# The load of W's first chunk: issued by ScalarE beside the first tile, in place of second on SyncE

## The chip, the cores and the metric

The kernel runs on one core of a Trainium2 chip. The metric is the device time of one execution in microseconds, as the median of several runs. The core has five engines that each follow their own list of instructions: TensorE (PE in the profile, with its weight loads as PEld), VectorE (DVE), ScalarE (ACT), GpSimd (POOL) and SyncE (SP), which here only issues transfers. Transfers between HBM and SBUF are carried by 16 DMA engines.

## The reference

The inputs are x (4 rows of 1024 positions with 512 features, f32), a condition of 256 numbers for each row, a matrix W of 1536 x 512 and a bias b of 512.

```python
def reference(x, cond, W, b):
    hidden = concat([cond, cond], -1)                      # (4, 512)
    x_mean = mean(x, axis=1, keepdims=True)                # (4, 1, 512)
    fused = concat([x, x_mean * ones, hidden[:, None] * ones], -1)
    return x + relu(einsum('bld,do->blo', fused, W) + b)
```

W has three parts of 512 rows. The first multiplies x itself, the second the mean over the positions, the third the condition. The last two give one vector for each of the four rows of x, which acts as a bias.

## The kernel before

**Tiling.** x is cut into 32 tiles of 128 positions, eight for each of the four rows. The part of W that multiplies x is cut into four chunks of 128 rows (j = 0 to 3). A chunk is a load of 256 KB: 128 partitions of 512 f32 numbers, one W row of 2 KB for each partition, and chunk j takes every fourth row beginning with row j. Tile 0 and tile 1 of x are also loaded alone, 256 KB each.

**Products.** Each operand is split in two numbers of a shorter type, a high part and what is left (hi and lo of x, w_hi and w_lo of W), and each tile takes three products for each chunk: hi by w_hi, lo by w_hi, hi by w_lo. So a tile needs 12 matmuls of 128 x 512 (L594), which add up in one PSUM bank.

**What the first tiles need.** Tiles of the first row of x are transposed by TensorE (`turn`, L427, four transposes for tile 0), then ScalarE makes hi (`split_hi`, L440) and VectorE makes lo (`split_lo`, L455) and the sums for the mean (`add_up`, L450). For each chunk of W, ScalarE or VectorE makes w_hi (`split_w_hi`, L398 or L400), and VectorE makes w_lo from it (`split_w_lo`, L403). Later rows of x are loaded in another layout (z, L334) and transposed by VectorE (L429).

**Order.** A planner (`Plan`) holds every step as a task with a cost on each engine that may do it, what it depends on and its due time. It draws an order for all engines by a search with a fixed seed and then emits each task in that order. All loads and stores are tasks of SyncE. The first loads have a fixed order in a list (`first_loads`):

```python
        (("x", 0, 0), 0.8, lambda e: load_x(0, 0, 1)),
        (("w", 0), 1.5, lambda e: load_w(0)),
        (("x", 0, 1), 1.0, lambda e: load_x(0, 1, 1)),
        (("w", 1), 0.9, lambda e: load_w(1)),
        (("w", 2), 0.7, lambda e: load_w(2)),
        (("w", 3), 0.7, lambda e: load_w(3)),
        (("x", 0, 2), 1.6, lambda e: load_x(0, 2, 2)),
```

Then follow the condition, b, tiles 4 to 7 of x in one load of 1 MB, and the z loads. In short, x0 and x1 here mean tiles 0 and 1 of x, and w0 to w3 the four chunks.

**Before the planned work.** Ahead of the planner's order the code emits some instructions by hand: VectorE clears a tile for warming (L266), ScalarE runs one Relu (L270), which brings the load of its function table with it, and TensorE multiplies zeros five times (`fill`, L278). More such fills are put in where the planner sees TensorE wait in the opening.

**Buffers.** x0 to x3 share one buffer of the pool `xpool` (five buffers, tag "x"), and the four chunks of W share the next one, `w_x`. Both are taken from the pool by the first load that writes them.

Of the kernel before, what the change touches and what calls it, by code (L numbers as in the profile page):

```python
# [9 lines left out]
F32 = mybir.dt.float32  # L10
# [201 lines left out]
def kernel(  # L212
# [8 lines left out]
    nc = tc.nc  # L221
    B, L, D = x.shape
    H = cond.shape[1]
    P = 128
    Q = 32
    NQ = P // Q
    J = D // P
# [5 lines left out]
    G = 4  # L233
# [12 lines left out]
    xpool = ctx.enter_context(tc.tile_pool(name="xpool", bufs=X_BUFS))  # L246
# [15 lines left out]
    Wv = W.rearrange("(s p j) o -> s p j o", p=P, j=J)  # L262
# [3 lines left out]
    nc.vector.memset(warm, 0.0)  # L266
    one = const.tile([P, 1], F32, name="one")
    nc.vector.memset(one, 1.0)
    table_warm = const.tile([P, 1], F32, name="table_warm")
    nc.scalar.activation(table_warm, one, AF.Relu)  # L270
    ident = const.tile([P, P], F32, name="ident")
# [41 lines left out]
    xs, zs, w_src = {}, {}, {}  # L313
# [3 lines left out]
    def load_x(g, i=0, n=G):  # L317
        r, k = divmod(g * G, NK)
        if not i:
            xs[g] = xpool.tile([P, G, D], F32, tag="x", name=f"x{g}")  # L320
        nc.sync.dma_start(out=xs[g][:, i : i + n], in_=xv[r, :, k + i : k + i + n, :])  # L321

    def x_tile(t):
# [14 lines left out]

    def load_w(j):
        if not j:  # L340
            w_src["x"] = xpool.tile([P, J, D], F32, tag="x", name="w_x")
        nc.sync.dma_start(out=w_src["x"][:, j, :], in_=Wv[0, :, j])

    def load_cond():
        w_src["cond"] = xpool.tile([P, 2, KH, D], F32, tag="x", name="w_cond")
# [5 lines left out]
    MB = 2.66  # L351
    first_loads = [
# [7 lines that stand above are left out]
        (("c",), 0.05, lambda e: nc.sync.dma_start(out=c_sb, in_=cond)),  # L360
        (("b",), 0.05, lambda e: nc.sync.dma_start(out=b_sb[0:1, :], in_=b.rearrange("(o d) -> o d", o=1))),
# [34 lines left out]
    def split_w_hi(e, j):  # L396
        if e == "act":
            nc.scalar.activation(w_hi[:, j, :], w_src["x"][:, j, :], AF.Copy)  # L398
        else:
            nc.vector.tensor_copy(w_hi[:, j, :], w_src["x"][:, j, :])  # L400

    def split_w_lo(e, j):
        nc_of[e].tensor_tensor(  # L403
            w_lo[:, j, :], w_src["x"][:, j, :], w_hi[:, j, :].bitcast(F32), ALU.subtract
        )

    for j in range(J):
        plan.add(("w_hi", j), {"act": (0.54, 0.63), "dve!": (0.37, 0.43)}, [("w", j)],
                 lambda e, j=j: split_w_hi(e, j))
        plan.add(("w_lo", j), {"dve!": (0.6, 0.69)}, [("w_hi", j)],  # L410
                 lambda e, j=j: split_w_lo(e, j))
# [323 lines left out]
```

## Time and profile before

| | before |
|---|---|
| median of 3 runs | 107.79 us (107.71 to 110.29) |
| the profiled execution's own time | 107.62 us |
| its span in the profile | 105.8 us |
| TensorE busy | 100.4 us (95%), 450 matmuls |
| VectorE, ScalarE, GpSimd busy | 79.9, 53.4, 63.8 us |
| moved by DMA | 26.31 MB, 249 GB/s over the span |
| granted TensorE clock | 1.0 in all 40 slices |

The span runs from the first to the last instruction that the profiler saw; 1.8 us of the execution's own time lie outside it. Lines such as L594 are lines of the kernel's file. SPq stands for the part of SyncE that issues transfers. A group's "busy" adds up its instructions, and the idle time after it is that of the engine just before them, with what ended it.

### The profile page before, as it was taken

Reading aid. Unit: us, or ns where it says so; the run is one execution under the profiler, and the core shown is the slowest. Engines: PE = TensorE matmul, PEld = TensorE weight load, DVE = VectorE, ACT = ScalarE, POOL = GpSimd, SP = SyncE. Lnnn points to the kernel's source line nnn. Section 1 sums busy time; section 2 is a strip of 40 time slices with the busy share of each in tenths; the row PEclk is TensorE's granted clock in tenths of the full one; section 3 lists DMA queues with packets and bytes.
Section 4 is the critical chain, followed back from the end, with each engine's and each line's share of the span. In section 5 each row is a group of like instructions: output and inputs, shape, how many; then the busy total and the mean of one; then the engine's idle time right before and its main releaser. Section 6 shows DMA issues by size and latency. Waiting matters only on the chain.

```text
span 105.8 us, 1452 instructions
## 1 busy us (share of the span) xinstructions
PE 100.4 (95%) x450; PEld 80.1 (76%) x450; DVE 79.9 (76%) x118; ACT 53.4 (50%) x121; POOL 63.8 (60%) x58
## 2 busy tenths in 40 slices
PE   5969999999999999999999999999999999999970
PEld 2447888888878878888878878888788788888860
DVE  1089154499999979999988999999998960488360
ACT  5253383572557482698665724776466220384000
POOL 6000000264040499999999999999999994087000
PEclk9999999999999999999999999999999999999999
DMA  2799999999999999992499999995699984004932
GB/s 108 180 386 396 270 204 286 427 271 201 266 299 192 201 202 201 200 293 96 163 239 253 330 392 390 390 405 212 218 264 345 349 318 184 20 6 192 344 147 104
DMA packets 22945, 26.31 MB, mean 249 GB/s; under 512 B 1173, under 2 KB 13721, under 8 KB 22810
## 3 DMA queue, kind: packets, MB, share of 16 engines
q1 hardware_dynamic: 22938, 26.23, 87.5%
q8 instruction: 3, 0.05, 0.2%
q14 instruction: 4, 0.03, 0.1%
HBM read 17.83 MB, written 8.39 MB: 248 GB/s over the span
## 4 chain that ended last, share of the span: by engine, by line
PE 89%; DMA 4%; DVE 2%; ACT 1%; SPq 0%; issue 0%
PE po_None L594 82%; DMA w_x<-in_L_cond_W_dram 4%; PE po L594 3%; PE xT L427 3%; PE pb L534 1%; PE pb L535 1%; DVE w_lo L403 1%; ACT w_hi L398 1%; DVE sums L450 1%; PE po L586 0%; DVE o L620 0%; SPq L321 0%; DVE w_hi L400 0%; PE pt L496 0%
## 5 line engine op out<-in xcount | busy, mean ns | idle before, releaser
L594 PE MATMUL po_None<-w_hi,hi 128*128 128x512 f32 x124 | 49.0, 399 | 1.0 <-ACT w_hi L398 0.7
L594 PE MATMUL po_None<-w_lo,hi 128*128 128x512 f32 x124 | 49.1, 399 | 0.0
L594 PE MATMUL po_None<-w_hi,lo 128*128 128x512 f32 x124 | 48.4, 397 | 0.0
L615 POOL TENSOR_TENSOR o<-o,x 128x512 f32<-128x512 f32 x27 | 34.7, 1317 | 4.5 <-ACT o L612 4.5
L594 PEld LDWEIGHTS po_None<-w_hi,hi 128*128 128x128 f32 x124 | 23.3, 188 | 7.2 <-ACT w_hi L398 1.4
L594 PEld LDWEIGHTS po_None<-w_lo,hi 128*128 128x128 f32 x124 | 23.3, 188 | 5.4 <-DVE w_lo L403 0.2
L440 ACT ACTIVATE hi<-xT 128x512 fp32r<-128x512 f32 (+1 forms) x34 | 19.8, 582 | 15.0 <-PE xT L427 8.1
L594 PEld LDWEIGHTS po_None<-w_hi,lo 128*128 128x128 f32 x124 | 23.3, 188 | 5.2
L429 DVE STREAM_TRANSPOSE xT<-z 128x512 f32<-128x512 f32 x24 | 25.5, 1093 | 1.4 <-POOL lo L455 1.4
L612 ACT ACTIVATE o<-o 128x512 f32<-128x512 f32 x30 | 17.9, 627 | 8.4 <-DVE o L609 3.9
L455 DVE TENSOR_TENSOR lo<-xT,hi 128x512 fp32r<-128x512 f32 (+1 forms) x22 | 14.0, 635 | 10.6 <-ACT hi L440 10.3
L455 POOL TENSOR_TENSOR lo<-xT,hi 128x512 fp32r<-128x512 f32 x12 | 15.5, 1299 | 9.5 <-ACT hi L440 9.5
L609 DVE TENSOR_TENSOR o<-po_None,bias 128x512 f32<-128x512 f32 x23 | 14.8, 680 | 7.0 <-ACT bias L539 4.7
L506 POOL TENSOR_TENSOR wc<-w_cond 128x512 f32<-128x512 f32 x2 | 2.6, 1298 | 18.2 <-DMA w_cond<-in_L_cond_W_dram 18.2
L520 DVE SCALAR_TENSOR_TENSOR acc<-w_mean,tot,acc 128x512 f32<-128x512 f32 x16 | 12.0, 751 | 0.4
L609 POOL TENSOR_TENSOR o<-o,bias 128x512 f32<-128x512 f32 x8 | 10.3, 1303 | 0.7 <-ACT bias L539 0.7
L605 ACT ACTIVATE o<-po_None 128x512 f32<-128x512 f32 x8 | 4.8, 596 | 6.1 <-PE po_None L594 6.1
L509 DVE SCALAR_TENSOR_TENSOR acc<-wc,cT,acc 128x512 f32<-128x512 f32 x8 | 5.9, 740 | 0.9 <-ACT acc L517 0.8
L427 PEld LDWEIGHTS xT<-ident,x 128*128 128x128 f32 x32 | 5.5, 205 | 1.3 <-issue 0.7
L440 ACT ACTIVATION_READ_ACCUMULATOR hi<-xT 128x1 f32 x32 | 6.2, 193 | 0.0
L526 ACT ACTIVATE acc_hi<-acc 128x512 fp32r<-128x512 f32 x4 | 2.4, 600 | 6.9 <-DVE acc L520 6.9
L539 ACT ACTIVATE bias<-pb 128x512 f32<-128x512 f32 x4 | 2.4, 600 | 6.8 <-PE pb L535 6.8
(44 smaller groups left out, 48.7 us busy)
## 6 DMA issues: line engine op xcount, KB each, us to landing
out_dram<-o SPq DMA_DIRECT2D x31, 256.0 KB, 3.9
x<-in_x_dram SPq DMA_DIRECT2D x7, 1024.0 KB, 8.4
z<-in_x_dram SPq DMA_DIRECT2D x24, 256.0 KB, 8.3
w_x<-in_L_cond_W_dram SPq DMA_DIRECT2D x4, 256.0 KB, 4.8
w_cond<-in_L_cond_W_dram SPq DMA_DIRECT2D x1, 1024.0 KB, 10.1
w_mean<-in_L_cond_W_dram SPq DMA_DIRECT2D x1, 1024.0 KB
x<-in_x_dram SPq DMA_DIRECT2D x2, 256.0 KB, 4.5
x<-in_x_dram SPq DMA_DIRECT2D x1, 512.0 KB, 6.0
```

Of the source, the lines that this page charges most:

```text
L427: nc.tensor.transpose(v[:, (m * n + i) * P : (m * n + i + 1) * P], x_t[:, j], ident)
L429: nc.vector.transpose(v[:, : n * P].rearrange("p (n t) -> p n t", t=Q), zs[u].rearrange("p n (a j) -> p n j a", j=J)[:, : n * NQ, js[0], :],)
L440: nc.scalar.activation(hi[c][:, :m], xT[c][:, :m], AF.Copy, accum_out=sums[:, r, js[0], s : s + 1] if units[u][2] > 1 else None,)
L455: nc_of[e].tensor_tensor(lo[c][:, :m], xT[c][:, :m], hi[c][:, :m].bitcast(F32), ALU.subtract)
L506: nc.gpsimd.tensor_tensor(wc[:, k], w_src["cond"][:, 0, k], w_src["cond"][:, 1, k], ALU.add)
L509: nc.vector.scalar_tensor_tensor(acc[r], wc[:, k], cT[:, k, r : r + 1], acc[r], ALU.mult, ALU.add)
L520: nc.vector.scalar_tensor_tensor(acc[r], w_mean[:, j, :], totals[r][:, j : j + 1], acc[r], ALU.mult, ALU.add)
L594: nc.tensor.matmul(v[:, : m.shape[-1]], lhsT=a, rhs=m, start=(t < LAST and i == 1), stop=(i == 3 * J),)
L605: nc.scalar.activation(o_tile(t), bank(t), AF.Copy)
L609: nc_of[e].tensor_tensor(o, o if t < PARK else bank(t), biases[t // NK], ALU.add)
L612: nc.scalar.activation(outs[t], outs[t], AF.Relu)
L615: nc_of[e].tensor_tensor(outs[t], outs[t], x_tile(t), ALU.add)
```

## The change

The buffers of x0 and of w0 are now taken from the pool at the start, in the same order as before. The load of w0 is emitted there too, by ScalarE and ahead of its Relu. The planner still has a task for w0 on SyncE with the same cost, but this task now emits nothing, so the order that the planner draws is the same, and all other loads keep their order on SyncE. The computation is not touched.

```diff
     one = const.tile([P, 1], F32, name="one")
     nc.vector.memset(one, 1.0)
+    x_0 = xpool.tile([P, G, D], F32, tag="x", name="x0")
+    w_x = xpool.tile([P, J, D], F32, tag="x", name="w_x")
+    nc.scalar.dma_start(out=w_x[:, 0, :], in_=Wv[0, :, 0])
     table_warm = const.tile([P, 1], F32, name="table_warm")
     nc.scalar.activation(table_warm, one, AF.Relu)
...
-            xs[g] = xpool.tile([P, G, D], F32, tag="x", name=f"x{g}")
+            xs[g] = xpool.tile([P, G, D], F32, tag="x", name=f"x{g}") if g else x_0
...
     def load_w(j):
         if not j:
-            w_src["x"] = xpool.tile([P, J, D], F32, tag="x", name="w_x")
-        nc.sync.dma_start(out=w_src["x"][:, j, :], in_=Wv[0, :, j])
+            w_src["x"] = w_x
+        else:
+            nc.sync.dma_start(out=w_x[:, j, :], in_=Wv[0, :, j])
```

## The prediction

> **What bounds the kernel now.** I read the page's busy times and the chain that ended last first. Chain columns: start, length, what ran.
>
> ```profile
> PE 100.4 (95%) x450; PEld 80.1 (76%) x450; DVE 79.9 (76%) x118; ACT 53.4 (50%) x121; POOL 63.8 (60%) x58
> 1.16 4.33 DMA w_x<-in_L_cond_W_dram
> 5.49 0.02 issue
> 5.51 0.64 ACT w_hi L398
> 6.15 0.02 issue
> 6.17 0.69 DVE w_lo L403
> 6.87 0.60 DVE sums L450
> 7.47 0.34 DVE w_hi L400
> 7.81 0.04 issue
> 7.86 4.72 PE po_None L594 x19
> ...
> 22.11 13.77 PE po_None L594 x59
> ...
> 101.11 1.43 PE po L594 x12
> ```
>
> From 7.86 us on the chain is TensorE alone up to its last matmul, 94.7 us later, so what happens in the opening moves the end one for one: each 0.1 us by which the product at 7.86 starts earlier or later is 0.1 us of the whole. Ahead of it the chain runs through the landing of w0 (5.49), ScalarE's w_hi (5.51), VectorE's w_lo (6.17), the sums (6.87) and VectorE's own w_hi of the next chunk (7.38). Everything that the change can do is decided there.
>
> Next the timeline of the opening, in which the two paths that meet at 6.17 can be told apart, and the chunk's time from issue to landing.
>
> ```profile
> 0.73 1.28 ACT L270 ACT_TABLE_LOAD   x1 [0.73 <-PEq L722]
> 0.74 0.37 SPq L321 DMA_DIRECT2D x<-in_x_dram  x1
> 1.16 0.42 SPq L342 DMA_DIRECT2D w_x<-in_L_cond_W_dram  x1
> 1.63 0.42 SPq L321 DMA_DIRECT2D x<-in_x_dram  x1
> 2.10 1.38 SPq L342 DMA_DIRECT2D w_x<-in_L_cond_W_dram  x3
> 3.31 1.10 PE L427 MATMUL xT<-ident,x 128*128 128x128 f32 x4
> 4.44 0.60 ACT L440 ACTIVATE hi<-xT 128x512 fp32r<-128x512 f32 x1 [2.22 <-PE xT L427]
> 5.07 0.69 DVE L455 TENSOR_TENSOR lo<-xT,hi 128x512 fp32r<-128x512 f32 x1 [3.86 <-ACT hi L440]
> 5.51 0.63 ACT L398 ACTIVATE w_hi<-w_x 128x512 fp32r<-128x512 f32 x1 [0.47 <-DMA w_x<-in_L_cond_W_dram]
> 6.17 0.69 DVE L403 TENSOR_TENSOR w_lo<-w_x,w_hi 128x512 fp32r<-128x512 f32 x1 [0.41 <-ACT w_hi L398]
> 6.78 0.69 DVE L450 TENSOR_REDUCE sums<-xT 128x4 f32<-128x512 f32 x1
> 7.38 0.42 DVE L400 CAST w_hi<-w_x 128x512 fp32r<-128x512 f32 x1
> DMA to landing us min/median/max: 4.3/4.8/5.1
> ```
>
> The x path: x0 is issued at 0.74, TensorE begins its transposes at 3.31, ScalarE makes hi at 4.44, VectorE makes lo at 5.07. The w path: w0 is issued at 1.16, lands at 5.49, and ScalarE makes w_hi at 5.51. VectorE issues operations of this kind 0.61 us apart (6.17 to 6.78), so after lo at 5.07 it is free for w_lo at 5.68, and it starts it at 6.17. **The x path thus has 0.49 us to spare, and the w path none.** That number is what the change can win at most, and it is also what it can take from x0 before it loses.
>
> w0 takes 4.33 us from issue to landing, though x0, issued by the same engine just before it, feeds a transpose 2.57 us after its own issue. The DMA traffic shows why (last columns: mean busy share of the DMA engines, above 1 with overlapping packets, and GB/s):
>
> ```profile
> 1.50:2.00 0.50, 0.50 (x2) 0.15 (x1) 0.00 (x0) 0.50 (x1) 0.44 (x3) 1.00 0.38 143
> 2.00:2.50 0.50, 0.50 (x3) 0.21 (x2) 0.00 (x0) 0.22 (x2) 0.26 (x1) 1.00 0.90 328
> 2.50:3.00 0.50, 0.50 (x3) 0.09 (x1) 0.00 (x0) 0.00 (x0) 0.00 (x0) 1.00 0.66 242
> 3.00:3.50 0.50, 0.50 (x3) 0.22 (x2) 0.00 (x0) 0.00 (x0) 0.00 (x0) 1.00 0.51 107
> 3.50:4.00 0.50, 0.50 (x4) 0.50 (x4) 0.00 (x0) 0.00 (x0) 0.00 (x0) 1.00 1.26 119
> 4.00:4.50 0.50, 0.50 (x3) 0.28 (x3) 0.00 (x0) 0.06 (x1) 0.00 (x0) 1.00 0.39 102
> 4.50:5.00 0.50, 0.50 (x2) 0.15 (x1) 0.00 (x0) 0.50 (x1) 0.00 (x0) 1.00 0.87 262
> 5.00:5.50 0.50, 0.45 (x2) 0.00 (x0) 0.43 (x1) 0.04 (x1) 0.00 (x0) 1.00 1.04 369
> 6.00:6.50 0.50, 0.31 (x1) 0.31 (x2) 0.33 (x1) 0.14 (x1) 0.00 (x0) 1.00 1.05 389
> ```
>
> x0's 262 kB are through by about 2.6 us: 72 kB (143 x 0.5), 164 kB, then 26 kB at 242 GB/s. Then comes a thin stretch: from 3.0 to 4.5 us only 102 to 119 GB/s, before the rate reaches 340 to 390 and stays there. It is just when w0 should move. The trace does not say whether w0 itself is slow to be read or whether anything would have been slow at that time. This is the largest unknown here.
>
> **The change part by part.** *The issue.* SyncE loses one issue, so w0 gets out at about 0.74 instead of 1.16, which is 0.42 us sooner, and x1, w1 and the rest each move up by about 0.47 (the step from 1.16 to 1.63). For these others it is worth at most that: at 340 to 390 GB/s from 5 us on the engines already have a backlog, and 262 kB at 390 GB/s take 0.67 us each, so they land in their old order at the pace of the DMA engines. The load of tiles 4 to 7 waits on SyncE for an earlier load:
>
> ```profile
> SPq L321 <- DMA w_x<-in_L_cond_W_dram: 0.7, 1, 0.7
> ```
>
> It would wait for x0 instead and be issued up to 0.7 us sooner, behind the loads already in line; I cost it at nothing, covered by that backlog.
>
> *ScalarE.* One issue is added ahead of the table load. By SyncE's rows it holds the sequencer for 0.37 to 0.43 us; the table load and the small Relu then end at about 2.65 instead of 2.22, and hi comes at 4.44, after 2.22 us of idle time in its row. Cost nothing, covered by this idle time; without it 0.42 us. The planner's order, the buffers and all later instructions stay, so nothing after 7.86 changes but by shifting.
>
> *w0's landing.* The trace has no load on ScalarE's queue. The bound on the good side is that it behaves like x0: data usable 2.57 us after issue, at 3.3. On the bad side it keeps its 4.33 us: 5.07. Both are good enough: w_hi needs ScalarE, which holds hi from 4.44, and two such operations follow each other 0.5 us apart, so w_hi could start at 4.94 to 5.09 and w_lo at 5.68 to 5.75. By itself this part is worth -0.42 to -0.49.
>
> *x0's landing.* What was two loads in line becomes two loads side by side on the same 16 engines. On the good side x0 still goes first and loses nothing: 0. On the bad side each packet of x0 waits for one of w0, and both end together. The two are 524 kB; 357 kB (72 + 164 + 121) moved by 3.0 us, and the missing 168 kB take 0.43 us at 389 GB/s, so x0 is through at 3.43 instead of 2.6: +0.83. Should the thin stretch stay where it is, the same 168 kB go at 102 to 119 GB/s and take 1.4 to 1.65 us, so x0 is through at 4.4 to 4.65: +1.8 to +2.05. I take +0.45, near the middle of the first two: the issues of two engines take 0.4 us each and need not start as one, and an x0 that leads by 0.4 us has half of its packets out before w0's come.
>
> The Trainium skill speaks against part of the hope here: its page "DMA: Bandwidth & Descriptors", section "Issuing engines are not separate DMA queues", says that transfers issued by several engines share the same 16 DMA engines and that a second issuer saves only the time to initiate. By this rule alone the sum would be the 0.42 us of the issue row, or 107.20 us for the profiled execution. No run here shows a second issuer yet; the rule and my sum differ by the packets that x0 has to let pass.
>
> *Sum.* w_lo can start when both paths are there: 5.68 + 0.45 = 6.13 by the x path, and 5.75 by the w path. That is 0.04 us before 6.17. Against the execution's own 107.62 us (span 105.8 and 1.8 around it) the sum is 107.58. The profiled execution lies 0.17 below the median of 107.79, so the same on the median's scale is 107.75, which I round to **107.7 us**.
>
> **The rivals.** *A, the forecast:* the path passes from w0 to x0, and most of what the earlier chunk gives is taken by the tile. x0's delay of 0.2 to 0.8 gives -0.29 to +0.31, or 107.5 to 108.1.
>
> *B, the gain comes through.* x0 is not disturbed, w0 is there by 5.1, and TensorE's product at 7.86 moves up by up to 0.49. For it speaks that w0 is the only wait on the w path; against it, that w1 to w3 then have to be there sooner as well. The landings run from 4.3 to 5.1 us after issues 0.47 apart, which puts the last, w3, at 8.2, and ScalarE works on w2 and w3 from 7.70. Where the backlog does not move up, that takes half of the gain. So -0.25 to -0.49: 107.3 to 107.5.
>
> *C, slower: the thin stretch holds the tile too.* If the low rate from 3.0 to 4.5 belongs to that time, or if slow reads of W stop the packets of x0 queued beside them, x0 comes 1.0 to 2.05 later. Its price is that delay less the 0.49 to spare: +0.5 to +1.56, or 108.3 to 109.35. It decides as soon as x0's transposes begin later than 3.80. For it speaks that the DMA engines' share is 0.51 and 0.39 in two of the thin rows and 1.26 in the third, with no more bytes: packets stood and did not move; against it, that x0 itself ran at 328 GB/s beside no such wait.
>
> *D, slower: TensorE's slow start lasts longer.* Its five fills, issued from 1.19, take 2.31 us in all, 0.46 each, and the three from 4.20 take 1.25, 0.42 each; the 59 matmuls that the chain has from 22.11 take 13.77, or 0.23 each:
>
> ```profile
> 1.19 2.31 PE L278 MATMUL pw<-warm 128*128 128x512 bf16 x5 [1.19 <-DVE one L268]
> 4.20 1.25 PE L278 MATMUL pw<-warm 128*128 128x512 bf16 x3
> ```
>
> TensorE is slow while it works from 1.19 to 5.45 without a pause, and fast at 7.86. A later x0 opens a pause ahead of the transposes. If this puts off the fast rate by another 4.3 us, then with matmuls at 0.43 instead of 0.23 about ten get done in which eighteen should, so 8 x 0.23 = 1.8 us are lost, on top of the path's own shift: about 109.4 to 110.1. Against it: the pause would be under a microsecond, and fills follow it. The Trainium skill's page "TensorE: Matmul & The Clock Gate", section "Part 1: The HAM clock gate", describes such a gate, which opens after a busy window that starts at no fixed point; the trace's slow start agrees, and no run here shows it delayed.
>
> *E, it does not do what it says.* The table load, 1.28 us at 0.73, could still run first on ScalarE. w0 would then be issued at 2.01, land 2.6 to 4.3 us later at 4.6 to 6.3, and the time would be 107.3 (the 0.49 in full) to 108.6 (0.8 later than now).
>
> **How the numbers follow.** I give A 0.46, B 0.22, C 0.20, D 0.06 and E 0.06. The predicted time is A's, 107.7. The range reaches from B's far end, less 0.2 for the spread of the shown runs, to the middle of C's upper half: 107.1 to 109.1. It leaves out D, the top of C and little else, under 2 in 10. About 2% is what a measurement of this kernel can tell from no change; that is 2.2 us, below 105.6 or above 109.95. No case gets to the first, since the opening has only 0.49 to give: 0.03, for what I have not seen. Above it lie a part of D and what C might do beyond its bounds: 0.07. Within it: 0.90.
>
> **What would show it.** In the changed kernel's timeline ScalarE has an issue ahead of its table load, and SyncE issues x1 at about 1.16. A is right if x0's transposes begin between 3.5 and 4.1 instead of 3.31 and VectorE's lo is followed by w_lo without a wait for W. B is right if they still begin by 3.4 and w_lo starts near 5.7. C is right if they begin after 4.2 and the windows from 3.0 to 4.5 are as thin as before. D shows as matmuls 0.43 us apart after the first product. I am wrong if the chain of TensorE after the first products gets a wait that it does not have now, or if w0 is still the last to arrive.

## The result, and the profile after

The changed kernel takes 109.35 us as the median of 22 runs (108.68 to 110.26), the kernel before 107.8 us in as many (107.43 to 110.8). The ratio is 1.0145, 95% interval [1.0124, 1.0165]: 1.5% slower, with an interval clear of no change, though less than the 2% that the prediction took for what a measurement can tell. Ratios here and below leave out executions 1.5% or more above the fastest of their kernel; medians don't. The forecast was 107.7 us, and the measured time lies above the range that was given, 107.1 to 109.1. The profiled execution took 108.69 us with a span of 106.9, at the low end of the 22 runs: it shows 1.07 us (from 107.62) of the 1.55 us by which the medians differ.

The chain that ended last, after the change (start, length, what ran):

```profile
0.74 3.99 DMA x<-in_x_dram
4.86 1.10 PE xT L431 x4
5.96 1.28 PE pw L281 x3
...
8.68 4.95 PE po_None L598 x21
...
23.18 13.77 PE po_None L598 x59
...
102.19 1.43 PE po L598 x12
```

Where the chain of before ran through the landing of w0, it now runs through the landing of x0. From 4.86 on it is all TensorE: from there on the chain's rows name no other engine and no transfer until its last matmul. The 59 matmuls that began at 22.11 now begin at 23.18 and take the same 13.77 us, so the whole loss of 1.07 us between the two profiles lies ahead of them.

The timeline of the opening:

```profile
0.73 0.40 ACTq L271 DMA_DIRECT2D w_x<-in_L_cond_W_dram  x1
0.74 0.84 SPq L324 DMA_DIRECT2D x<-in_x_dram  x2
1.17 1.28 ACT L273 ACT_TABLE_LOAD   x1 [1.17 <-PEq L726]
4.86 1.10 PE L431 MATMUL xT<-ident,x 128*128 128x128 f32 x4 [1.36 <-DMA x<-in_x_dram]
6.00 0.60 ACT L444 ACTIVATE hi<-xT 128x512 fp32r<-128x512 f32 x1 [3.34 <-PE xT L431]
6.49 0.62 ACT L402 ACTIVATE w_hi<-w_x 128x512 fp32r<-128x512 f32 x1
6.63 0.69 DVE L459 TENSOR_TENSOR lo<-xT,hi 128x512 fp32r<-128x512 f32 x1 [5.42 <-ACT hi L444]
7.24 0.68 DVE L407 TENSOR_TENSOR w_lo<-w_x,w_hi 128x512 fp32r<-128x512 f32 x1
7.76 0.92 PE L431 MATMUL xT<-ident,x 128*128 128x128 f32 x4
8.44 0.42 DVE L404 CAST w_hi<-w_x 128x512 fp32r<-128x512 f32 x1
8.91 0.19 PEld L598 LDWEIGHTS po_None<-w_hi,hi 128*128 128x128 f32 x1 [0.20 <-DVE w_hi L404]
8.99 0.42 PE L598 MATMUL po_None<-w_hi,hi 128*128 128x512 f32 x1
```

ScalarE issues w0 at 0.73, in the same moment as SyncE issues x0. w_hi at 6.49 has no wait for W in its row: it follows hi (6.00) at once, so w0 is no longer the last to arrive. x0 is: its transposes begin at 4.86 and not at 3.31, and TensorE's row names the transfer of x that it waited for. The steps behind it keep the distances of before, 1.14 us to hi and 0.63 to lo; w_lo follows lo after 0.61 without a wait, where before it waited for w0. The weights of the product at 8.99 still wait for VectorE's w_hi, as before, so this path and TensorE's own chain (transposes, three fills, product, transposes) end within 0.1 us of each other here.

The windows of the same stretch (last columns: share of the DMA engines, GB/s):

```profile
1.50:2.00 0.50, 0.50 (x2) 0.15 (x1) 0.00 (x0) 0.50 (x1) 0.44 (x3) 1.00 0.48 90
2.00:2.50 0.50, 0.50 (x3) 0.21 (x2) 0.00 (x0) 0.49 (x2) 0.27 (x1) 1.00 0.44 156
2.50:3.00 0.50, 0.50 (x3) 0.10 (x1) 0.00 (x0) 0.16 (x1) 0.00 (x0) 1.00 0.39 102
3.00:3.50 0.50, 0.50 (x2) 0.00 (x0) 0.00 (x0) 0.00 (x0) 0.00 (x0) 1.00 0.92 344
3.50:4.00 0.50, 0.00 (x1) 0.00 (x0) 0.00 (x0) 0.00 (x0) 0.00 (x0) 1.00 1.10 307
4.00:4.50 0.50, 0.00 (x0) 0.00 (x0) 0.00 (x0) 0.00 (x0) 0.00 (x0) 1.00 0.85 197
```

The thin stretch did not stay at 3.0 to 4.5. It now lies up to 3.0, just where x0 had run at 328 and 242 GB/s, and 3.0 to 3.5 moves 344 GB/s. Most of it moved with w0; a shorter one is left at 4.0 to 4.5 (197 GB/s).

### The profile page after: what moved, and what is told of

It is laid out like the page before. It is cut to its first block, busy times and chain, and to the rows that moved or that the text cites. A ratio compares the mean times of both kernels' runs of the same rounds, so it can differ in the third digit from the quotient of the medians.

```text
span 106.9 us, 1452 instructions
## 1 busy us (share of the span) xinstructions
PE 101.1 (95%) x450; PEld 80.4 (75%) x450; DVE 79.8 (75%) x118; ACT 53.3 (50%) x121; POOL 63.8 (60%) x58
## 4 chain that ended last, share of the span: by engine, by line
PE 92%; DMA 4%; DVE 0%; issue 0%
PE po_None L598 82%; PE xT L431 4%; DMA x<-in_x_dram 4%; PE po L598 3%; PE pw L281 1%; PE pb L538 1%; PE pb L539 1%; PE po L590 0%; DVE o L624 0%; PE pt L500 0%
## 5 line engine op out<-in xcount | busy, mean ns | idle before, releaser
L431 PE MATMUL xT<-ident,x 128*128 128x128 f32 x32 | 6.1, 311 | 1.4 <-DMA x<-in_x_dram 1.4
```

Of the source, the lines that this page charges most:

```text
L431: nc.tensor.transpose(v[:, (m * n + i) * P : (m * n + i + 1) * P], x_t[:, j], ident)
```

## The experiments

Theory 1, formed on these windows: W's first reads are slow wherever they stand, and while they are pending, packets of other loads on the same DMA engines wait too. The rivals were that the second load of the opening is slow whatever it reads, and that a second issuer at the start is what holds up x0. All ratios are to the kernel before, run on the same chip beside them; there its median was 108.05 to 108.8 us.

**x1 as the second load, w0 as the third, all on SyncE.**

```diff
-        (("w", 0), 1.5, lambda e: load_w(0)),
-        (("x", 0, 1), 1.0, lambda e: load_x(0, 1, 1)),
+        (("w", 0), 1.5, lambda e: load_x(0, 1, 1)),
+        (("x", 0, 1), 1.0, lambda e: load_w(0)),
```

> All loads on SyncE as before, but x1 is the second load and w0 the third. Theory 1: the first reads of W are slow, wherever they stand, and hold up what is queued on the same DMA engines. Then the windows from 2.5 to 3.5 us run at 300 GB/s or more and the thin stretch (100 to 160 GB/s) begins only behind x1, near 3.3 to 3.5; w0 lands at 5.5 to 6.1, time 107.8 to 108.5 us. Theory 2: the second load of the opening is slow, whatever it reads. Then the windows from 3.0 to 4.5 are as thin as before (102 to 119 GB/s), x1 lands at 5.5 and w0 0.67 later, time 108.3 to 108.6.

Measured: 109.21 us, ratio 1.0078 [1.0031, 1.0125]. Its windows:

```profile
2.50:3.00 0.50, 0.50 (x3) 0.09 (x1) 0.00 (x0) 0.00 (x0) 0.00 (x0) 1.00 1.03 373
3.00:3.50 0.50, 0.50 (x2) 0.00 (x0) 0.00 (x0) 0.00 (x0) 0.00 (x0) 1.00 1.03 401
...
4.00:4.50 0.50, 0.50 (x4) 0.50 (x4) 0.00 (x0) 0.00 (x0) 0.00 (x0) 1.00 1.02 148
4.50:5.00 0.50, 0.50 (x5) 0.24 (x3) 0.00 (x0) 0.25 (x1) 0.00 (x0) 1.00 0.78 156
```

The second load, x1, runs at 373 and 401 GB/s, and the thin stretch follows it. Being second is not what makes a load slow. w0 landed at 6.35 us and the time is 109.21, both later than theory 1 had them.

**The second load from x's place, not from W.**

```diff
-        nc.sync.dma_start(out=w_src["x"][:, j, :], in_=Wv[0, :, j])
+        nc.sync.dma_start(out=w_src["x"][:, j, :], in_=Wv[0, :, j] if j else xv[0, :, 0, :])
```

> As before, but the second load reads the place of x's tile 0 again in place of chunk 0 of W (so the products of chunk 0 use other numbers). Theory 1: the second load then runs at 300 GB/s or more, lands by 4.0, and the thin stretch comes with w1, the fourth load, from about 4 us; w1 lands near 7 or later; time 107.3 to 108.5. Theory 2: thin from 3.0 to 4.5 as before, the second load lands at 5.3 to 5.6, time 107.6 to 107.9.

Measured: 108.02 us, 0.9964 [0.9916, 1.0013].

```profile
3.00:3.50 0.50, 0.50 (x3) 0.07 (x1) 0.00 (x0) 0.00 (x0) 0.00 (x0) 1.00 1.06 389
...
4.50:5.00 0.50, 0.50 (x3) 0.16 (x2) 0.00 (x0) 0.40 (x1) 0.00 (x0) 1.00 0.74 172
```

With the same destination and place in line, the load of 3.0 to 3.5 runs at 389 GB/s where w0 got 107. The rate falls to 172 later, when w1 reads W for the first time, though not as low as 102 to 119. So what is slow lies at the source, W, and not in the buffer or the queue. (The rows read here had just been read by x0; x1 in the run above is read for the first time and is as fast.)

**w0 ahead of x0 on SyncE.**

The buffers are taken at the start as in the changed kernel, but ScalarE issues nothing.

```diff
...
-        (("x", 0, 0), 0.8, lambda e: load_x(0, 0, 1)),
-        (("w", 0), 1.5, lambda e: load_w(0)),
+        (("x", 0, 0), 0.8, lambda e: load_w(0)),
+        (("w", 0), 1.5, lambda e: load_x(0, 0, 1)),
```

> All loads on SyncE, w0 issued first and x0 second. Theory 1 (the first reads of W are slow wherever they stand): under 200 GB/s from 1.7 to about 3.5 us, w0 lands at 4 to 4.8, x0 behind it is late, transposes at 4.4 to 5.2; time +0.6% to +1.4%. Rival (whichever tensor is read second in the opening is slow, the first one's slow touch is hidden ahead of its first packet): the first 262 kB go at 300 GB/s or more, the thin stretch hits x0 instead, transposes at 5.0 to 5.6; time +1.2% to +2%.

Measured: 109.79 us, 1.0129 [1.0077, 1.0182].

```profile
2.50:3.00 0.50, 0.50 (x3) 0.10 (x1) 0.00 (x0) 0.00 (x0) 0.00 (x0) 1.00 0.33 102
3.00:3.50 0.50, 0.50 (x2) 0.00 (x0) 0.00 (x0) 0.00 (x0) 0.00 (x0) 1.00 0.56 127
```

W is slow as the very first load too (102 and 127 GB/s), and x0 behind it has its transposes only at 5.66, later than the 4.4 to 5.2 that theory 1 had.

**ScalarE issues x1, not w0, beside x0.**

```diff
+    x_0 = xpool.tile([P, G, D], F32, tag="x", name="x0")
+    nc.scalar.dma_start(out=x_0[:, 1:2], in_=xv[0, :, 1:2, :])
     table_warm = const.tile([P, 1], F32, name="table_warm")
...
-        (("x", 0, 1), 1.0, lambda e: load_x(0, 1, 1)),
+        (("x", 0, 1), 1.0, lambda e: None),
```

> ScalarE's first instruction loads x1 beside x0 on SyncE; w0 stays on SyncE, now as its second load. Theory 1 (first reads of W are slow and hold up their neighbours): x0 only shares with x1, and W's reads start behind x0, so x0's transposes begin between 3.4 and 4.1 us, the windows before 2.5 run at 300 GB/s or more, the thin stretch follows; time 107.6 to 108.5. Theory 2 (a second load beside or behind the first is slow, whatever it reads; two issuers at once are slow in the opening): transposes at 4.5 to 4.9 and windows from 1.5 to 3.0 at 90 to 160 GB/s as in the changed kernel; time 108.7 to 109.4.

Measured: 108.94 us, 0.9998 [0.9938, 1.0058]. Its timeline and windows:

```profile
4.05 1.10 PE L429 MATMUL xT<-ident,x 128*128 128x128 f32 x4 [0.54 <-DMA x<-in_x_dram]
```

```profile
2.50:3.00 0.50, 0.50 (x3) 0.10 (x1) 0.00 (x0) 0.16 (x1) 0.00 (x0) 1.00 0.98 365
3.00:3.50 0.50, 0.50 (x2) 0.00 (x0) 0.00 (x0) 0.00 (x0) 0.00 (x0) 1.00 1.05 389
...
4.00:4.50 0.50, 0.45 (x2) 0.48 (x3) 0.00 (x0) 0.00 (x0) 0.00 (x0) 1.00 0.84 143
```

Two issuers at once do not slow the engines from 2.5 on: 365 and 389 GB/s. The windows before that, expected at 300 GB/s or more, ran at 49 and 266. x0 is still late, at 4.05, with x1 beside it, and the thin stretch comes with w0 behind them. The time, above the range that was expected, says little of x0: w0 is last again here, and w_hi waits for it until 6.21.

**The changed kernel again, and with its one load taken from x's place.** The second of these differs from the changed kernel by one source:

```diff
-    nc.scalar.dma_start(out=w_x[:, 0, :], in_=Wv[0, :, 0])
+    nc.scalar.dma_start(out=w_x[:, 0, :], in_=x[0, :P, :])
```

> The changed kernel once more, on the chip of the runs beside it, to see how late x0 comes where W is read beside it. Theory 1 (the first reads of W are slow and hold up x0's packets on the same engines): x0's transposes begin at 4.5 to 5.3 us, well behind the 4.05 of x1 beside x0, and the thin stretch (under 200 GB/s) lies before 3.5. Rival: W only shares, and the first profile was a chance; then they begin at 3.8 to 4.2 and the time is within 0.5% of before.

> The changed kernel with one edit: ScalarE's load reads the place of x's tile 0 in place of chunk 0 of W (so the products of chunk 0 use other numbers). Theory 1 (the first reads of W are slow and hold up x0's packets): x0 now only shares, its transposes begin at 3.8 to 4.2 us as with x1 beside it, against 4.86 and 5.21 in the changed kernel; the thin stretch comes with w1. Time 0.5% to 1.5% below the changed kernel. Rival (a second issuer at the start is what holds up x0): transposes at 4.7 to 5.3 and under 200 GB/s from 1.5 to 3.0 again.

Measured: the changed kernel 109.14 us, 1.0128 [1.0082, 1.0174]; with the other source 108.53 us, 1.0017 [0.9978, 1.0057]. Three views of the changed kernel, x0's transposes, a window and a row of its chain:

```profile
5.21 1.10 PE L431 MATMUL xT<-ident,x 128*128 128x128 f32 x4 [1.71 <-DMA x<-in_x_dram]
```

```profile
2.50:3.00 0.50, 0.50 (x3) 0.10 (x1) 0.00 (x0) 0.16 (x1) 0.00 (x0) 1.00 0.35 119
```

```profile
23.60 13.77 PE po_None L598 x59
```

The first two with the load from x's place:

```profile
4.28 1.10 PE L431 MATMUL xT<-ident,x 128*128 128x128 f32 x4 [0.77 <-DMA x<-in_x_dram]
```

```profile
2.50:3.00 0.50, 0.50 (x3) 0.09 (x1) 0.00 (x0) 0.16 (x1) 0.00 (x0) 1.00 1.02 377
```

One source makes 119 GB/s or 377 in this window, and 5.21 or 4.28 for x0 (just above the 3.8 to 4.2 that was expected). Nearly all of the loss goes with it. The two were not run side by side, so the time's step, 1.1%, is that of two ratios to before. The execution profiled here took 109.10 us, near the median, and its 59 matmuls begin at 23.60: 1.49 us later than before, and the execution is 1.48 us longer. So the larger loss lies in the opening too. The windows before 2.5 do not tell the two sources apart: 45 and 131 GB/s with W, 49 and 135 with x.

How x0 is held up can be read from the packets of 1.5 to 3.0 us by queue (packets, MB, share of the 16 engines' time). q1 is SyncE's, q10 ScalarE's, which in these kernels carries the one load beside x0 and nothing else. In the first profile of the changed kernel:

```profile
q1 hardware_dynamic: 64, 0.13, 35.1%
q10 hardware_dynamic: 21, 0.04, 8.6%
```

and with the load from x's place:

```profile
q1 hardware_dynamic: 81, 0.17, 57.2%
q10 hardware_dynamic: 56, 0.11, 20.6%
```

With W beside it, x0's queue is behind although w0's moved only 21 packets. So x0 does not lose its turns to packets of w0: both queues move less, and by the shares the engines carry a packet for 44% of the time, against 78% with x. What holds them up, the trace does not say.

**The changed kernel with W read in one piece, and its partner without the second issuer.** Each chunk is 128 rows that follow each other, in place of every fourth row of 1 MB:

```diff
-    nc.scalar.dma_start(out=w_x[:, 0, :], in_=Wv[0, :, 0])
+    nc.scalar.dma_start(out=w_x[:, 0, :], in_=W[:P])
...
-            nc.sync.dma_start(out=w_x[:, j, :], in_=Wv[0, :, j])
+            nc.sync.dma_start(out=w_x[:, j, :], in_=W[j * P : (j + 1) * P])
```

> The changed kernel with each chunk of W read as 128 rows that follow each other (256 KB in one piece; other numbers in the products). W is still read beside x0 by a second issuer. Theory 1 (the slow first reads of a chunk spread over 1 MB hold up x0): with the reads in one piece x0 mainly shares, transposes at 3.9 to 4.5 us and not 4.86 to 5.21; time 0.7% to 1.5% below the changed kernel, that is within 0.4% of before, and above the kernel before with W in one piece (0.987), whose x0 goes alone. Rival (any read of W beside x0 does it): transposes at 4.7 or later, time 1% or more above before.

> The kernel before with each chunk read as 128 rows that follow each other (256 KB in one piece) and not every fourth row of 1 MB (other numbers in the products). If the slow first reads grow with the region that a load spreads over, w0 lands by 4.9 us and w1 to w3 each pay a part, so that w3 lands as late as before or later. If they don't, w0 lands at 5.2 to 5.7 as before and the time is within 0.4% of before.

> The kernel before with W in one piece once more, on the same chip as the run beside it: 0.985 to 0.991 of before.

Measured: with the second issuer 108.23 us, 1.0045 [1.0007, 1.0082]; without it 107.32 us, 0.9869 [0.9823, 0.9915], and beside the other 107.4 us, 0.9959 [0.9925, 0.9993]. That second value missed what was expected of it (0.985 to 0.991). With the second issuer:

```profile
4.28 1.10 PE L431 MATMUL xT<-ident,x 128*128 128x128 f32 x4 [0.79 <-DMA x<-in_x_dram]
```

```profile
2.50:3.00 0.50, 0.50 (x3) 0.09 (x1) 0.00 (x0) 0.15 (x1) 0.00 (x0) 1.00 0.91 340
3.00:3.50 0.50, 0.50 (x2) 0.00 (x0) 0.00 (x0) 0.00 (x0) 0.00 (x0) 1.00 1.04 406
```

Without it, run beside:

```profile
3.60 0.93 PE L427 MATMUL xT<-ident,x 128*128 128x128 f32 x4
```

W beside x0 gives 4.28 here, just as x beside x0 did, and 340 and 406 GB/s; the ratio, 1.0045, lies a little outside the 0.4% that was expected. So it isn't any read of W that holds up x0 so long, but the reads spread over 1 MB. Whether the size of that region or the step of four rows does it, these runs do not separate. What is left, 3.60 to 4.28, is the price of sharing in this pair: 0.68 us. It is known to a few tenths only, for in the six profiles where x0 goes first and nothing is issued beside it, its transposes begin anywhere from 3.31 to 3.75.

**ScalarE's issue behind the Relu.** The line of the load was moved behind the line of the Relu.

> The changed kernel with w0's issue on ScalarE behind the table load and the Relu, at about 2.2 us. Both theories: x0 goes alone, its transposes begin at 3.3 us as before. Theory 1: W's first reads come from x1's neighbour w1 on SyncE or from w0, near 3.2, thin from there, w0 lands at 5.2 to 6.8; time 107.4 to 109. Theory 2: x1 as the second load is slow, thin from 2.75 as before and w0 behind it at 5.5 to 6.5; time 107.8 to 108.8. If x0 is late here too (after 3.8), neither holds and it is the second queue itself.

Measured: 109.37 us, 1.0111 [1.0053, 1.0169].

```profile
0.73 1.28 ACT L272 ACT_TABLE_LOAD   x1 [0.73 <-PEq L726]
1.20 0.38 ACTq L273 DMA_DIRECT2D w_x<-in_L_cond_W_dram  x1
3.74 1.10 PE L431 MATMUL xT<-ident,x 128*128 128x128 f32 x4 [0.23 <-DMA x<-in_x_dram]
6.48 0.63 ACT L402 ACTIVATE w_hi<-w_x 128x512 fp32r<-128x512 f32 x1 [1.00 <-DMA w_x<-in_L_cond_W_dram]
```

The premise failed: the load came out at 1.20, while the table load ran until 2.01 and the Relu behind it had not begun. So this run has w0 half a microsecond behind x0. x0 is spared (3.74, within the 3.31 to 3.75 of x0 without a load issued beside it), and w0, now sharing with x1, is last again: w_hi waits for it until 6.48. The time is above the 107.4 to 109 that theory 1 had.

**A first touch of W's rows.** Three runs of the kernel before with a small added load by ScalarE's first instruction into a tile that nobody uses: 16 bytes of each row of w0 (twice), and 16 bytes of 17 rows over one DMA engine.

```diff
+    touch = const.tile([P, 4], F32, name="touch")
+    nc.scalar.dma_start(out=touch, in_=Wv[0, :, 0, :4])
     table_warm = const.tile([P, 1], F32, name="table_warm")
```

> The kernel before, with one added load that ScalarE issues as its first instruction: 16 bytes of each of the 128 rows that w0 will read, into a tile that nobody uses. Theory 1a (slow is only the first touch of these places, and any read of them pays for it): w0's own reads then run at 250 GB/s or more between 3.0 and 4.5 us and w0 lands by 4.7; x0's packets pay a part, transposes at 3.4 to 4.3; time from -0.4% to +0.8% of before. Theory 1b (W's reads are slow for longer, touch or no touch): thin stretch from 3.0 to 4.5 as before, w0 lands at 5.3 or later, time +0% to +1%.

> The added 16-byte reads of w0's rows once more, with more rounds, since the first run gave 0.9941 [0.9891, 0.9990] though w0 still landed at 5.4 us. If the touch takes something off the slow reads (it lies off the chain of the median run and shortens the bad ones), the ratio is 0.993 to 0.998 again; if that was a draw of chance, 0.999 to 1.004.

> The kernel before, with one added load by ScalarE as its first instruction: 16 bytes of 17 rows of W, 60 KB apart over the 1 MB that w0 reads from, which go over a single DMA engine. If the first touch warms something that all DMA engines share, w0 lands by 4.7 us and x0's transposes begin at 3.3 to 3.9, since at most one of 16 engines is held up; time -0.5% to 0%. If what is slow belongs to each engine or to each row, w0 lands at 5.3 or later as before, time within 0.3% of before.

Measured: 107.82 us, 0.9941 [0.9891, 0.9990]; again 107.96 us, 0.9975 [0.9938, 1.0011]; over one engine 108.69 us, 1.0000 [0.9956, 1.0045]. With the rows touched, the windows are these:

```profile
3.50:4.00 0.50, 0.31 (x3) 0.34 (x3) 0.00 (x0) 0.00 (x0) 0.00 (x0) 1.00 1.00 197
4.00:4.50 0.50, 0.50 (x4) 0.50 (x3) 0.00 (x0) 0.00 (x0) 0.00 (x0) 1.00 0.87 160
4.50:5.00 0.50, 0.50 (x3) 0.17 (x2) 0.00 (x0) 0.17 (x1) 0.00 (x0) 1.00 0.94 156
```

These windows are less thin than the 102 to 119 GB/s of before, but far from the 250 GB/s or more that was expected if the touch pays for all, and w_hi comes at 5.37 (5.45 with the touch over one engine, 5.51 before). So a touch of 16 bytes for each row does not take the slowness away. Whether it wins some tenths of a per cent is not settled by an interval that reaches to 1.0011.

**The second load from W's third part.**

```diff
-        nc.sync.dma_start(out=w_src["x"][:, j, :], in_=Wv[0, :, j])
+        nc.sync.dma_start(out=w_src["x"][:, j, :], in_=Wv[0, :, j] if j else Wv[2, :, 0])
```

> The kernel before, but the second load reads the first chunk of W's third part (rows 1024 on) in place of chunk 0 (other numbers in those products). If it is the first read of the tensor W that is slow, whatever its place, the thin stretch is at 3.0 to 4.5 as before and w1 follows 0.7 us behind the second load. If each region pays for itself, there are two thin stretches: one for the second load and another when w1 first reads part one; w1 then lands 1.5 us or more behind x1, and the time is 0.5% to 1.5% above before.

Measured: 110.68 us, 1.0148 [1.0076, 1.0221]. The profiled execution took 111.68 us and is read for its opening only:

```profile
3.50:4.00 0.50, 0.41 (x3) 0.44 (x3) 0.00 (x0) 0.00 (x0) 0.00 (x0) 1.00 0.66 143
...
5.00:5.50 0.50, 0.28 (x2) 0.00 (x0) 0.20 (x1) 0.50 (x2) 0.00 (x0) 1.00 1.11 344
...
6.50:7.00 0.50, 0.50 (x5) 0.50 (x5) 0.50 (x2) 0.00 (x0) 0.00 (x0) 1.00 0.74 172
```

There are two thin stretches with 344 GB/s between them, the second when w1 first reads part one. This is what each region paying for its first read would look like; it rests on this one opening.

## Why the prediction was wrong

*The bound and the 0.49 us to spare: right.* In the first profile x0's transposes came 1.55 us later; less 0.49 that is 1.06. The product that began at 7.86 begins at 8.99, 1.13 later, and the execution's time rose by 1.07, from 107.62 to 108.69. In the second, x0 came 1.90 later; less 0.49 that is 1.41, and the time rose by 1.48. One for one, within 0.1 us.

*The issue and ScalarE: right.* The issue came out at 0.73 ahead of the table load (rival E falls), and ScalarE's delay is covered. The load of tiles 4 to 7 did not go out 0.7 us sooner but at 5.44 against 5.50, for now the load of b ahead of it waits 1.0 us for W; it was costed at nothing, and the chain has no wait for it.

*w0's landing: right in what it does.* w_hi has no wait for W any more. The path passed from w0 to x0, as case A said.

*x0's landing: here it failed.* The term was +0.45, "near the middle of the first two", 0 and +0.83. It measured +1.55, and +1.90 in the second profile. The step that failed is the count behind these bounds, that 357 kB would have moved by 3.0 us and the rest would follow at 389 GB/s: it took over the rates that x0 had in before, with w0 behind it, for a start with w0 beside it. The windows of the changed kernel give 45 + 78 + 51 = 174 kB by 3.0 us, half as much; with x's place read beside x0 they give 24 + 68 + 188 = 280.

Two things were mis-sized. First, sharing alone costs near the upper of the two bounds: 0.68 us in the pair run side by side, and 4.05 with x1 beside x0 is 0.74 behind the 3.31 of before. The reason I gave for the middle, that x0 would lead by 0.4 us, fell with two issues at 0.73 and 0.74; the moved issue at 1.20, with x0 at 3.74, shows what such a lead would have been worth. Second, the thin stretch was not part of the likeliest case at all. I bounded it as staying at 3.0 to 4.5 and left open whether it belonged to w0. It belongs to w0, came forward with it, and x0's queue moves little while it lasts: 4.86 and 5.21 against 4.05 to 4.28 where what is read beside x0 isn't W spread over 1 MB, which is 0.6 to 1.2 us more.

*Rival C is what happened*, by the second of its two conditions, "if slow reads of W stop the packets of x0 queued beside them". Its point of decision, transposes later than 3.80, its delay of 1.0 to 2.05 us and its price, up to 109.35 us, hold; the windows that it named do not. I gave it 0.20 and ended the range inside it. The windows of before did speak for it more than I let them: x0 ran at 328 GB/s until its bytes were nearly through, and the rate fell as w0's turn came.

*Rival D: at most 0.07 us.* TensorE is slow for longer (tile 1's transposes take 0.92 where they took 0.64), but of the 1.13 us only 0.07 are not x0's. The granted clock stands at 1.00 in every window shown, before and after, so the slow start shows in the durations of the matmuls alone, and no run here says what it comes from. *Rival B* falls with x0's delay.

*The rule on issuers.* The Trainium skill's page "DMA: Bandwidth & Descriptors", section "Issuing engines are not separate DMA queues", says that loads of several issuers interleave on the same engines. The run with x1 beside x0 agrees: 365 to 389 GB/s in all, x0 0.74 later than before. The other half, that a second issuer saves the issue time, gave 107.20 us; the measured execution took 108.69, because x0, which was the more urgent once w0 was early, paid for it.

## What to carry to other kernels

A transfer that is last on the chain isn't freed by issuing it beside the one that is needed just before it: here both then ended together (x0 landed at 4.73 us, and w0's queue moved its last packets after 4.5), and the first user waited for both. Before moving a slow load earlier, find out whether its slowness belongs to its place in time or to its source, by giving it another source at the same place or another load its place; in the second case it takes the slow stretch with it, onto whatever stands beside it. And count the slack of the path that will have to wait, here 0.49 us, before counting the gain.

## What was not expected of the hardware

- The first reads of a region of W run at about 100 to 170 GB/s for 1 to 2 us, and later chunks of the same 1 MB at 340 to 400. The Trainium skill's page "DMA: Bandwidth & Descriptors", section "Latency and other measured facts", has copies that lose rate by a large row pitch; here w1 to w3 have w0's pitch, 8 KB, and the window from 6.0 to 6.5 of before has 389 GB/s, so the pitch alone is not it. Why the first reads are slow stays open. x's first load did not show it in the kernel before (143 and 328 GB/s from 1.5 to 2.5), but it did in others: 33 and 193 with x1 as the second load, 49 and 135 with two loads of x's place side by side. There it is over by 2.5, with 373 and 377 GB/s next. So a slow start is not W's alone; W's is longer.
- Chunk 0 of W in one piece is there sooner: w_hi begins at 5.19 and 5.06 without a wait for W, before at 5.51 with one. The time is 0.9869 [0.9823, 0.9915] and 0.9959 [0.9925, 0.9993] of before. That is not yet a better kernel, for the features of x would have to be dealt out in the same order, and the z loads, whose pieces are now 128 features long, would be cut into pieces of 32; this wasn't tried.
- A load that stands behind the table load and the Relu in ScalarE's list was issued at 1.20 us, while the table load ran from 0.73 to 2.01.
